# A hybrid transformer block: the first attention's rotated keys turned on VectorE through DRAM, two weight loads issued by ScalarE, input rows loaded a group earlier, and normalisation transposes of the feed-forward pinned in order

## The chip, the cores and the metric

The kernel runs on one core of a Trainium2 chip, in one launch. The metric is the device time of that launch in microseconds, lower is better. Three runs of the kernel before took 2479.9, 2481.11 and 2481.55 us; the median, 2481.11 us, is the time before. The profile is of one more execution, which took 2478.19 us.

Engines: PE (TensorE: matmuls, and transposes by a matmul with the identity), DVE (VectorE), ACT (ScalarE), POOL (GpSimd) and SP (SyncE, which here only issues DMAs). SBUF is the on-chip memory, with 128 partitions; PSUM holds what PE writes, in banks of 128 x 512 floats. All data are fp32.

## The reference

Four layers with residuals act on `x` of shape (4, 512, 512), that is 4 batches of 512 rows:

```python
x = x + attn_a(layernorm(x), Wq, Wk, Wv, Wo)      # "first attention"
x = x + ffn(layernorm(x), w1, w2, w3)             # ternary weights
x = x + attn_b(layernorm(x), codes, scales, ...)  # "second attention"
x = x + ffn(layernorm(x), w1, w2, w3)             # the same weights again
```

The change is in the first attention, and a little in the feed-forward. The first attention has 16 query heads and 4 key/value heads of 128:

```python
q, k, v = h @ Wq, h @ Wk, h @ Wv          # k, v repeated for 4 query heads each
o_gla = scan(S = S * exp(gl_t) + softmax(k)_t v_t;  o_t = softmax(q)_t S)
        # gl = log_sigmoid(k) / 16
sq, sk = rotary(q), rotary(k)
y = softmax(causal(sq @ sk.T / sqrt(128))) @ v
out = (0.5 * y + 0.5 * o_gla) @ Wo
```

## The kernel before, in words

**Groups and chunks.** The first attention works through 16 groups, one for each batch `b` and key head `g`, in the order `b`-major: group m has (b, g) = divmod(m, 4). A group has 4 chunks of 128 rows. So there are 64 chunks, and `step(n)` (L550) runs once for each chunk number n from -7 to 65. It is a software pipeline: in one step the parts of several chunks are traced, in the order in which L550 to L617 list them. With `m, p = divmod(n + 7, 4)`, `p` says at which quarter of the preparation of group m the step is. For a chunk c of a group, the parts are:

- `A` (L447): the query projection, 4 matmuls in PSUM tag `mm`, copied to `q_t` by ACT. `B` (L453): the decayed softmax of q (`qd`), its turning on its side, and the rotation (`qr`). `C` (L471): `qr` transposed by PE. `D(h)` (L482): scores of head h against the rotated keys `krT` in PSUM tag `sc`, masked maximum by DVE (L492), exponential by ACT (L495), division by ACT (L497), turning by DVE (L498); after head 3 the result is written to DRAM. `E` (L503) reads it back. `own` (L475) and `F` (L510) make the output, `G` (L522) multiplies it by Wo and adds it to the residual rows `xs` (L191, DVE).
- A group's preparation is spread over `part(m, p, half)` (L528): p = 0, 1 project k and v and start the gates; p = 2 `decays` (L405), in which DVE and POOL also make the rotated keys `kr` (L421 to 422) and then `kd`; p = 3 `transposes` (L426), in which PE transposes `kr` and `kd`, 4 blocks of 128 x 128 each (L362), and ACT copies both out of PSUM, `krT` with the factor 1/sqrt(128) (L428); p = 4 `states`. The chunk that first uses `krT` comes three steps after `transposes`.

**Turning through DRAM.** VectorE's transpose turns only blocks of 32 x 32. The kernel uses it on `qd` already: `turned` (one buffer) gets the turned blocks (L459), one DMA writes it to DRAM (`queries`, L461, 256 KB), and one step later four DMAs read it back (L468), each for the 32 partitions of one quarter, so that the blocks land transposed. The probabilities take the same way (L498, L501, L507).

**Loads.** SP issues nearly all DMAs, in one in-order queue. `load(b)` (L105) fetches the four tiles of input rows of batch b, at p = 0 of the last group of the batch before (L554 to 556: steps 5, 21 and 37). `load_wq` (L382) and `load_wo` (L386) fetch 1 MB each for a group; their tiles have one buffer, so they wait for the last matmul that reads the old weights.

**Layernorm.** `layernorm_steps` (L123) is a generator, advanced a bit at a time inside the steps: statistics of the rows by DVE (L132, L133), the scale by POOL and DVE (L138 to L145), the normalised rows `xn` (L160, one buffer), four PE transposes (L165) and a copy out. For the first attention, `normalise(b + 1)` starts one step after `load(b + 1)`. `halved` (L172) does the same for the two feed-forwards, with the result split in two fp32r halves; there the batch b + 1 is normalised while batch b is multiplied (L1086, L1100 to 1101).

**What sets the order.** The instructions are traced in program order, and a list scheduler then orders each engine's instructions by its own estimate of times: an instruction that it believes to be ready may be put ahead of others that were traced earlier. Two things hold it back. Inside the steps 0 to 63 PE's order is exactly the traced one (`manual_schedule`, L622), for the instructions traced there. And `in_place` (L79) pins one instruction behind whatever was traced before it on its engine. The order that comes out is fixed in the program; on the chip each engine's queue is in order, and an instruction that waits holds up those behind it. PSUM tags `mm` and `tp` have two banks, `sc` three.

Of the kernel before, what the change touches and what calls it, by code (L numbers as in the profile page):

```python
# [9 lines left out]
F32 = mybir.dt.float32  # L10
# [9 lines left out]
P = 128  # L20
B, S, C = 4, 512, 512
NC = S // P
# [52 lines left out]
def hybrid_block(ctx: ExitStack, tc: tile.TileContext, a: dict, out: bass.AP):  # L75
# [42 lines left out]
    def split(hi, lo, src, engine=nc.vector):  # L118

        nc.scalar.copy(hi, src)  # L120
        engine.tensor_tensor(lo, src, hi, ALU.subtract)

    def layernorm_steps(b, sink, tag="tp", apart=False):  # L123

        mv = lnp.tile([P, NC, 2], F32, tag="mv", name="mv")
        rstd = lnp.tile([P, NC], F32, tag="rstd", name="rstd")

        def moments(c):  # L130
            st = lnp.tile([P, 6], F32, tag="st", name="st")
            nc.vector.bn_stats(st, xs[b * NC + c])  # L132
            nc.vector.bn_aggr(mv[:, c, :], st)  # L133

        def scales(at):

            var = lnp.tile([P, NC], F32, tag="var", name="var")[:, at]
            nc.vector.tensor_scalar(var, mv[:, at, 1], LN_EPS, None, ALU.add)  # L138
            r = rstd[:, at]
            nc.gpsimd.tensor_tensor(r, var, power[:, : r.shape[1]], ALU.pow)  # L140
            t = lnp.tile([P, NC], F32, tag="newton", name="newton")[:, at]
            nc.vector.tensor_tensor(t, r, r, ALU.mult)
            nc.vector.tensor_tensor(t, t, var, ALU.mult)
            nc.vector.tensor_scalar(t, t, -0.5, 1.5, ALU.mult, ALU.add)
            nc.vector.tensor_tensor(r, r, t, ALU.mult)  # L145

        if not apart:
            for c in range(NC):
                moments(c)
                if c == 1:  # L150
                    yield
            scales(slice(0, NC))
        for c in range(NC):
            if apart:
                moments(c)
                scales(slice(c, c + 1))
            else:
                yield
            xn = lnp.tile([P, C], F32, tag="xn", name="xn", bufs=1)
            nc.vector.tensor_scalar(xn, xs[b * NC + c], mv[:, c, 0:1], rstd[:, c : c + 1], ALU.subtract, ALU.mult)  # L160
            if not apart:
                yield
            tp = bank(tag, [P, NK, P])
            for k in range(NK):
                nc.tensor.transpose(tp[:, k, :], xn[:, k * P : (k + 1) * P], ident)  # L165
            sink(c, tp)

    def layernorm(b, sink, tag="tp", apart=False):
        for _ in layernorm_steps(b, sink, tag, apart):
            pass  # L170

    def halved(pool, b):  # L172

        halves = [pool.tile([P, NK, S], F32R, tag=f"xn{n}", name=f"xn{n}") for n in ("hi", "lo")]
        return halves, layernorm_steps(b, lambda c, tp: split(*(h[:, :, c * P : (c + 1) * P] for h in halves), tp))

    def whole(pool, b):

# [130 lines left out]
    def first_attention_gentle(base, extra):  # L309
# [6 lines left out]
        with ExitStack() as st:  # L316
# [41 lines left out]
            def transposed(dst, src, engine):  # L358

                tp = bank("tp", [P, 4, P])  # L360
                for i in range(4):
                    nc.tensor.transpose(tp[:, i, :], src[:, i, :], ident)  # L362
                engine(dst, tp)

            xnTs = {}

            def normalise(b, apart=False):
# [4 lines left out]
            class Group:  # L372
# [8 lines left out]

                def load_wq(self):  # L382
                    self.wq = one.tile([P, NK, HG * D], F32, tag="wq", name="wq")
                    nc.sync.dma_start(self.wq, a["Wq"][:, self.g * HG * D : (self.g + 1) * HG * D].rearrange("(k p) n -> p k n", p=P))

                def load_wo(self):  # L386
                    self.wo = late.tile([P, HG, C], F32, tag="wo", name="wo")
                    nc.sync.dma_start(self.wo, a["Wo"][self.g * HG * D : (self.g + 1) * HG * D, :].rearrange("(h p) n -> p h n", p=P))

                def project(self, c):  # L390
                    acc = bank("mm", [P, 2, D])
# [13 lines left out]
                def decays(self):  # L405

                    dec = bank("mm", [P, NC, D])
                    halves = [one.tile([P, NC, D], F32R, tag=tag, name=f"gate{x}") for x, tag in (("hi", "held"), ("lo", "kd"))]
                    split(*halves, self.gate)
                    project(dec.rearrange("p c d -> p (c d)"), lambda i: until, lambda i: halves[i].rearrange("p c d -> p (c d)"), 2)  # L410

                    held = one.tile([P, NC, D], F32, tag="held", name="held")
                    nc.vector.tensor_scalar(held, dec, -2.0 * GENTLE * GATE_NORM, None, ALU.max)
                    self.down = two.tile([P, NC, D], F32, tag="down", name="down")
                    nc.scalar.activation(self.down, held, AF.Exp, scale=1.0 / GATE_NORM)
                    self.ends = two.tile([P, NC - 1], F32, tag="ends", name="ends")
                    for c in range(NC - 1):
                        nc.sync.dma_start(self.ends[:, c : c + 1], self.down[P - 1 : P, c, :])
                    n = self.g * B + self.b
                    nc.scalar.activation(held, held, AF.Exp, scale=-1.0 / GATE_NORM, accum_out=steep[:, n : n + 1])  # L420
                    self.kr = one.tile([P, NC, D], F32, tag="gate", name="kr")  # L421
                    rotate(self.kr, self.k_t, turn[:, :, 0:1, :], turn[:, :, 1:3, :])
                    self.kd = one.tile([P, NC, D], F32, tag="kd", name="kd")
                    softmax_decayed(self.kd, self.k_t, lambda c: held[:, c, :])

                def transposes(self):  # L426
                    self.krT = two.tile([P, S], F32, tag="krT", name="krT")
                    transposed(self.krT.rearrange("p (c t) -> p c t", c=NC), self.kr, lambda o, i: nc.scalar.mul(o, i, SCALE))  # L428
                    self.kdT = two.tile([P, NC, P], F32, tag="kdT", name="kdT")
                    transposed(self.kdT, self.kd, nc.scalar.copy)  # L430

# [11 lines left out]
            class Chunk:  # L443
# [9 lines left out]
                def B(self):  # L453
                    c = self.c
                    qd = one.tile([P, HG, D], F32, tag="qd", name="qd")
                    softmax_decayed(qd, self.q_t, lambda h: self.k.down[:, c, :])

                    turned = one.tile([P, 4, HG, 32], F32, tag="turned", name="turned")
                    nc.vector.transpose(turned.rearrange("p q h t -> p h q t"), qd.rearrange("p h (q j) -> p h q j", q=4))  # L459
                    self.queries = dram.tile([P, HG * D], F32, tag="queries", name="queries", bufs=3)  # L460
                    in_place(nc.sync.dma_start(self.queries, turned.rearrange("p q h t -> p (q h t)")))  # L461
                    self.qr = two.tile([P, HG, D], F32, tag="qr", name="qr")
                    rotate(self.qr, self.q_t, turn[:, c : c + 1, 0:1, :], turn[:, c : c + 1, 1:3, :])

                def L(self):
                    qdT = two.tile([P, 4, HG, 32], F32, tag="qdT", name="qdT", bufs=4)
                    for q in range(4):
                        in_place(nc.sync.dma_start(qdT[32 * q : 32 * (q + 1)].rearrange("j a h t -> j a (h t)"), self.queries.rearrange("(a j) (q x) -> q j a x", a=4, q=4)[q]))  # L468
                    self.qdT = qdT.rearrange("p a h t -> p h a t")

                def C(self):  # L471
# [10 lines left out]
                def D(self, h):  # L482
# [2 lines left out]
                    if h == 0:  # L485
                        self.turned = late.tile([P, HG * P * (3 + c % 2)], F32, tag=f"turned{c % 2}", name="turned")[:, : 4 * HG * 32 * n]
                    sc = bank("sc", [P, 4, 32 * n])
                    nc.tensor.matmul(sc.rearrange("p q (k j) -> p q k j", j=32), lhsT=self.qrT[:, h, :], rhs=self.k.krT.rearrange("p (k q j) -> p q k j", q=4, j=32)[:, :, :n, :], start=True, stop=True)  # L488
                    nm = two.tile([P, 1], F32, tag="nm", name="nm", bufs=4)
                    flat = sc.rearrange("p q x -> p (q x)")  # L490

                    nc.vector.tensor_tensor_reduce(sc, sc, causal[:, :, 32 * (3 - c) :], -1.0, 3e38, ALU.add, ALU.min, nm)  # L492
                    pr = two.tile([P, S], F32, tag="pr", name="pr", bufs=5)[:, : P * n]
                    den = two.tile([P, 1], F32, tag="den", name="den", bufs=4)
                    nc.scalar.activation(pr, flat, AF.Exp, bias=nm, scale=-1.0, accum_out=den)  # L495
# [54 lines left out]
            def step(n):  # L550
                nonlocal ln
                m, p = divmod(n + 7, NC)
                at = lambda i: chunks.get(n + i) if n + i < last else None
                if (m + 1) % KV == 0 and (m + 1) // KV < B:  # L554
                    if p == 0:
                        load((m + 1) // KV)
                    if p == 1:
                        ln = normalise((m + 1) // KV)
                    if p > 1:
                        next(ln)  # L560
# [514 lines left out]
    def feed_forward(base, last, first):  # L1075

        with ExitStack() as st:
# [5 lines left out]
            ws = [block((soon, soon) if f < 2 else pools, f) for f in range(NF)]  # L1083
            xn = first
            for b in range(B):
                ready, steps = halved(base, b + 1) if b + 1 < B else (None, iter(()))  # L1086
                hid = []
                for f, (w, _) in enumerate(ws):
                    xs12 = []
# [102 lines left out]
```

## Time and profile before

| | us |
|---|---|
| median of 3 runs | 2481.11 (2479.9 to 2481.55) |
| the profiled execution | 2478.19 |
| its span, first to last instruction | 2476.4 |
| PE busy in the span | 2427.4 (98%) |
| DVE, ACT, POOL busy | 1648.0 (67%), 1209.7 (49%), 387.7 (16%) |
| mean granted TensorE clock | 0.994 |
| first attention, from 0 to its last residual addition (L191) | 0 to 1053.3 |

How to read it: "busy" is the time in which an engine had an instruction under way; matmuls overlap a little with the next, so for PE the start of the next instruction says what one really costs. A timeline row gives the start in us, the duration in us, engine, line, operation, out<-in, and how many like instructions are merged in it (an fp32 matmul stands as two records, so four matmuls show as x8; a transpose stands as one). In square brackets stands how long the engine sat idle before the row, and what ended that. PE's clock is granted by a throttle; after an idle stretch the same matmuls can run slower for a while. SPq and ACTq are the DMAs that SP and ACT issue.

### The profile page before, as it was taken

The numbers are of one execution on the slowest core, as the hardware profiler recorded it, in microseconds if no ns is written. First come the engines' busy times: TensorE is split into PE (matmuls) and PEld (weight loads), VectorE is DVE, ScalarE is ACT, GpSimd is POOL, SyncE is SP. The second block draws the span as 40 slices with busy tenths as digits, with TensorE's granted clock in tenths as the row PEclk, the third lists the DMA queues.
The fourth block names the chain that finished last, engine by engine and source line by source line (L and its number), as shares of the span: only waits on it lengthen the run. The fifth ranks groups of instructions, "written<-read, shape, count | busy, mean of one in ns | idle before, by whom it ended". The sixth has DMA issues, their size and how long they took to land.

```text
span 2476.4 us, 28996 instructions
## 1 busy us (share of the span) xinstructions
PE 2427.4 (98%) x8552; PEld 1544.3 (62%) x8552; DVE 1648.0 (67%) x3816; ACT 1209.7 (49%) x3066; POOL 387.7 (16%) x424
## 2 busy tenths in 40 slices
PE   7999999999999999899999999999999999999998
PEld 4545555555555555477886666666666666668887
DVE  6778777887878888456558666666766666664332
ACT  5756665666666665233326554444444444432222
POOL 1222222122222222022223333100000000000000
PEclk9999999999999999899999999999999999999999
DMA  4667765776656655475436777544343434333000
GB/s 146 190 176 208 209 190 176 206 208 181 187 174 196 196 176 165 127 230 149 128 107 187 200 185 221 146 115 116 94 131 93 125 93 132 89 92 132 18 18 19
DMA packets 240615, 367.10 MB, mean 148 GB/s; under 512 B 41664, under 2 KB 126912, under 8 KB 234304
## 3 DMA queue, kind: packets, MB, share of 16 engines
q1 hardware_dynamic: 231088, 338.58, 48.2%
q0 software_dynamic: 7680, 25.17, 3.5%
q8 instruction: 71, 1.16, 0.2%
q10 hardware_dynamic: 1680, 1.39, 0.2%
q14 instruction: 96, 0.79, 0.1%
HBM read 209.53 MB, written 88.34 MB: 120 GB/s over the span
## 4 chain that ended last, share of the span: by engine, by line
PE 89%; DVE 5%; issue 2%; ACT 1%; DMA 1%; SPq 1%; POOL 1%; DVEq 0%; POOLq 0%; ACTq 0%
PE mm L186 44%; PE sc L186 13%; PE sc L888 9%; PE pv L518 5%; PE sc L488 5%; PE pv L922 4%; PE tp L922 4%; PE sc L478 2%; PE pv L516 1%; PE tp L362 1%; PE tp L165 1%; SPq L915 1%; DVE st L132 0%; DVE xn L160 0%; DMA prT<-turned 0%
## 5 line engine op out<-in xcount | busy, mean ns | idle before, releaser
L893 ACT ACTIVATE pr<-sc,nm 128x512 f32<-128x512 f32 x256 | 175.8, 687 | 302.6 <-DVE nm L890 259.2
L186 PE MATMUL sc<-xnhi,block 128*128 128x512 f32 x704 | 276.9, 393 | 2.1 <-ACT hT L1095 2.1
L186 PE MATMUL sc<-xnlo,block 128*128 128x512 f32 x704 | 274.3, 390 | 0.0
L888 PE MATMUL sc<-kT,qT 128*128 128x512 f32 x512 | 262.0, 594 | 0.6 <-ACT kT L870 0.6
L186 PE MATMUL mm<-xnhi,w 128*128 128x512 f32 x512 | 254.1, 496 | 0.0
L186 PE MATMUL mm<-wq,xnT 128*128 128x512 f32 x512 | 232.2, 596 | 4.1 <-DVE x L191 2.0
L186 PE MATMUL mm<-wo,oT 128*128 128x512 f32 x512 | 232.8, 598 | 1.1 <-ACT oT L520 0.7
L890 DVE TENSOR_REDUCE nm<-sc 128x1 f32<-128x512 f32 x256 | 174.9, 683 | 74.3 <-PE sc L888 72.1
L186 PE MATMUL mm<-xnlo,w 128*128 128x512 f32 x512 | 205.9, 402 | 0.0
L910 DVE STREAM_TRANSPOSE turned<-pr 128x512 f32<-128x512 f32 x256 | 173.4, 696 | 37.0 <-ACT pr L900 34.0
L343 POOL TENSOR_TENSOR sw<-q_t,turn 128x256 f32<-128x256 f32 x128 | 98.8, 792 | 510.6 <-ACT q_t L451 441.2
L900 ACT ACTIVATE pr<-pr,den 128x512 f32<-128x512 f32 x192 | 138.2, 722 | 82.6 <-DVE den L898 82.6
L488 PE MATMUL sc<-krT,qrT 128*128 128x512 f32 (+3 forms) x512 | 170.4, 433 | 2.2 <-ACT pr L495 2.2
L497 ACT ACTIVATE pr<-pr,den 128x128 f32<-128x128 f32 (+3 forms) x256 | 141.7, 558 | 48.2 <-DVE den L496 46.3
L186 PEld LDWEIGHTS mm<-wq,xnT 128*128 128x128 f32 x512 | 96.4, 191 | 109.9 <-issue 99.1
L495 ACT ACTIVATE pr<-sc,nm 128x128 f32<-128x128 f32 (+3 forms) x256 | 132.6, 519 | 65.2 <-DVE nm L492 55.5
L498 DVE STREAM_TRANSPOSE turned<-pr 128x128 f32<-128x128 f32 (+3 forms) x256 | 128.6, 504 | 47.4 <-ACT pr L497 43.0
L186 PEld LDWEIGHTS mm<-wo,oT 128*128 128x128 f32 x512 | 96.8, 192 | 101.3 <-issue 96.0
L186 PEld LDWEIGHTS sc<-xnhi,block 128*128 128x128 f32 x704 | 132.2, 188 | 31.1 <-ACT hT L1095 2.9
L186 PEld LDWEIGHTS sc<-xnlo,block 128*128 128x128 f32 x704 | 132.2, 188 | 27.7 <-issue 0.7
L518 PE MATMUL pv<-prT,v_t 128*128 128x512 f32 x320 | 147.8, 592 | 0.0
L888 PEld LDWEIGHTS sc<-kT,qT 128*128 128x128 f32 x512 | 95.8, 189 | 81.6 <-issue 63.5
(151 smaller groups left out, 4801.5 us busy)
## 6 DMA issues: line engine op xcount, KB each, us to landing
prT<-turned SPq DMA_DIRECT2D x1024, 64.0 KB, 2.0
w<-exact SPq DMA_DIRECT2D x32, 1024.0 KB, 5.3
wq<-in_Wq SPq DMA_DIRECT2D x16, 1024.0 KB, 5.7
wo<-in_Wo SPq DMA_DIRECT2D x16, 1024.0 KB, 5.9
queries<-turned SPq DMA_DIRECT2D x64, 256.0 KB, 2.3
qdT<-queries SPq DMA_DIRECT2D x256, 64.0 KB, 3.0
passed<-turned SPq DMA_DIRECT2D x16, 1024.0 KB, 4.3
prT<-passed SPq DMA_DIRECT2D x64, 256.0 KB, 5.9
```

The source lines that it names most:

```text
L186: nc.tensor.matmul(acc, lhsT=lhs(k), rhs=rhs(k), start=k == 0, stop=k == n - 1)
L488: nc.tensor.matmul(sc.rearrange("p q (k j) -> p q k j", j=32), lhsT=self.qrT[:, h, :], rhs=self.k.krT.rearrange("p (k q j) -> p q k j", q= ...
L495: nc.scalar.activation(pr, flat, AF.Exp, bias=nm, scale=-1.0, accum_out=den)
L497: nc.scalar.mul(pr, pr, den)
L498: nc.vector.transpose(self.turned.rearrange("p (q h x) -> p q h x", q=4, h=HG)[:, :, h, :], pr.rearrange("p (q x) -> p q x", q=4))
L518: nc.tensor.matmul(acc.rearrange("p h (a t) -> p h a t", a=4), lhsT=self.k.v_t[:, j, :], rhs=self.wts[:, :, :, j, :], start=j == c == 0, s ...
L888: nc.tensor.matmul(sc, lhsT=qTs[u][:, i * P : (i + 1) * P], rhs=kTs[u], start=True, stop=True)
L890: nc.vector.tensor_reduce(nm, sc, AX.X, ALU.max, negate=True)
L893: nc.scalar.activation(pr, sc, AF.Exp, bias=nm, accum_out=den)
L900: nc.scalar.mul(pr, pr, den)
L910: nc.vector.transpose(turns[u][:, :, i, :], pr.rearrange("p (q k) -> p q k", q=4))
L922: nc.tensor.matmul(accs[u].rearrange("p (n t) -> p n t", t=32), lhsT=v_ts[m, j][:, h * D : (h + 1) * D], rhs=prTs[u].rearrange("p a i (k t ...
```

## The change

- **Rotated keys.** `kr` is no longer transposed by PE. `decays` turns it in blocks on DVE into `turned` (the same single buffer that the queries use) and has SP write it to DRAM; `transposes` has SP read it back with four DMAs. The two helpers `blocks_to_dram` and `quarters` hold what L459 to L461 and L467 to L468 did for the queries, and serve both. `krT` is thereby stored by quarters, and is no longer scaled: the factor goes into the masked maximum of L492, which takes -1/sqrt(128) where it took -1. The DRAM tag `queries` has four buffers in place of three.
- **Wq and Wo** of the first attention are issued by ACT, each pinned behind the ACT instruction traced before it, in place of SP.
- **Input rows** of the next batch are loaded at p = 0 of the second last group of a batch: steps 1, 17 and 33 in place of 5, 21 and 37.
- **Transposes held.** In the feed-forwards, the first of the four transposes of each chunk of the next batch's normalisation is pinned behind the PE instruction traced before it.

```diff
-    def layernorm_steps(b, sink, tag="tp", apart=False):
+    def layernorm_steps(b, sink, tag="tp", apart=False, place=lambda i: i):
...
             for k in range(NK):
-                nc.tensor.transpose(tp[:, k, :], xn[:, k * P : (k + 1) * P], ident)
+                t = nc.tensor.transpose(tp[:, k, :], xn[:, k * P : (k + 1) * P], ident)
+                if k == 0:
+                    place(t)
...
-    def halved(pool, b):
+    def halved(pool, b, **kw):
...
-        return halves, layernorm_steps(b, lambda c, tp: split(*(h[:, :, c * P : (c + 1) * P] for h in halves), tp))
+        return halves, layernorm_steps(b, lambda c, tp: split(*(h[:, :, c * P : (c + 1) * P] for h in halves), tp), **kw)
...
+            def blocks_to_dram(src):
+
+                turned = one.tile([P, 4, 4, 32], F32, tag="turned", name="turned")
+                nc.vector.transpose(turned.rearrange("p q n t -> p n q t"), src.rearrange("p n (q j) -> p n q j", q=4))
+                to = dram.tile([P, 4 * P], F32, tag="queries", name="queries", bufs=4)
+                in_place(nc.sync.dma_start(to, turned.rearrange("p q n t -> p (q n t)")))
+                return to
+
+            def quarters(dst, src):
+
+                for q in range(4):
+                    in_place(nc.sync.dma_start(dst[32 * q : 32 * (q + 1)].rearrange("j (a x) -> j a x", a=4), src.rearrange("(a j) (q x) -> q j a x", a=4, q=4)[q]))
...
-                    nc.sync.dma_start(self.wq, a["Wq"][:, self.g * HG * D : (self.g + 1) * HG * D].rearrange("(k p) n -> p k n", p=P))
+                    in_place(nc.scalar.dma_start(self.wq, a["Wq"][:, self.g * HG * D : (self.g + 1) * HG * D].rearrange("(k p) n -> p k n", p=P)))
...
-                    nc.sync.dma_start(self.wo, a["Wo"][self.g * HG * D : (self.g + 1) * HG * D, :].rearrange("(h p) n -> p h n", p=P))
+                    in_place(nc.scalar.dma_start(self.wo, a["Wo"][self.g * HG * D : (self.g + 1) * HG * D, :].rearrange("(h p) n -> p h n", p=P)))
...
-                    self.kr = one.tile([P, NC, D], F32, tag="gate", name="kr")
-                    rotate(self.kr, self.k_t, turn[:, :, 0:1, :], turn[:, :, 1:3, :])
+                    kr = one.tile([P, NC, D], F32, tag="gate", name="kr")
+                    rotate(kr, self.k_t, turn[:, :, 0:1, :], turn[:, :, 1:3, :])
+                    self.keys = blocks_to_dram(kr)
...
-                    self.krT = two.tile([P, S], F32, tag="krT", name="krT")
-                    transposed(self.krT.rearrange("p (c t) -> p c t", c=NC), self.kr, lambda o, i: nc.scalar.mul(o, i, SCALE))
+                    krT = two.tile([P, S], F32, tag="krT", name="krT")
+                    quarters(krT, self.keys)
+                    self.krT = krT.rearrange("p (q k j) -> p q k j", q=4, j=32)
...
-                    nc.vector.tensor_tensor_reduce(sc, sc, causal[:, :, 32 * (3 - c) :], -1.0, 3e38, ALU.add, ALU.min, nm)
+                    nc.vector.tensor_tensor_reduce(sc, sc, causal[:, :, 32 * (3 - c) :], -SCALE, 3e38, ALU.add, ALU.min, nm)
...
+                if p == 0 and (m + 2) % KV == 0 and (m + 2) // KV < B:
+                    load((m + 2) // KV)
                 if (m + 1) % KV == 0 and (m + 1) // KV < B:
-                    if p == 0:
-                        load((m + 1) // KV)
...
-                ready, steps = halved(base, b + 1) if b + 1 < B else (None, iter(()))
+                ready, steps = halved(base, b + 1, place=in_place) if b + 1 < B else (None, iter(()))
```

More of the change, by code (lines that the diff above doesn't have):

```diff
@@ L456, in B @@
                     softmax_decayed(qd, self.q_t, lambda h: self.k.down[:, c, :])
[L458 to L461, printed above, removed]
+                    self.queries = blocks_to_dram(qd)
                     self.qr = two.tile([P, HG, D], F32, tag="qr", name="qr")
@@ L466, in L @@
                     qdT = two.tile([P, 4, HG, 32], F32, tag="qdT", name="qdT", bufs=4)
-                    for q in range(4):
-                        in_place(nc.sync.dma_start(qdT[32 * q : 32 * (q + 1)].rearrange("j a h t -> j a (h t)"), self.queries.rearrange("(a j) (q x) -> q j a x", a=4, q=4)[q]))
+                    quarters(qdT.rearrange("p a h t -> p (a h t)"), self.queries)
                     self.qdT = qdT.rearrange("p a h t -> p h a t")
@@ L487, in D @@
                     sc = bank("sc", [P, 4, 32 * n])
-                    nc.tensor.matmul(sc.rearrange("p q (k j) -> p q k j", j=32), lhsT=self.qrT[:, h, :], rhs=self.k.krT.rearrange("p (k q j) -> p q k j", q=4, j=32)[:, :, :n, :], start=True, stop=True)
+                    nc.tensor.matmul(sc.rearrange("p q (k j) -> p q k j", j=32), lhsT=self.qrT[:, h, :], rhs=self.k.krT[:, :, :n, :], start=True, stop=True)
                     nm = two.tile([P, 1], F32, tag="nm", name="nm", bufs=4)
                     flat = sc.rearrange("p q x -> p (q x)")
-                    nc.vector.tensor_tensor_reduce(sc, sc, causal[:, :, 32 * (3 - c) :], -1.0, 3e38, ALU.add, ALU.min, nm)
+                    nc.vector.tensor_tensor_reduce(sc, sc, causal[:, :, 32 * (3 - c) :], -SCALE, 3e38, ALU.add, ALU.min, nm)
                     pr = two.tile([P, S], F32, tag="pr", name="pr", bufs=5)[:, : P * n]
```

## The prediction

> **What bounds the kernel now.** I read the shares by engine first, then the chain that ended last by engine, then a 50 us stretch of the first attention by windows, because the edits lie in that stage.
>
> ```profile
> PE 2427.4 (98%) x8552; PEld 1544.3 (62%) x8552; DVE 1648.0 (67%) x3816; ACT 1209.7 (49%) x3066; POOL 387.7 (16%) x424
> PE 89%; DVE 5%; issue 2%; ACT 1%; DMA 1%; SPq 1%; POOL 1%; DVEq 0%; POOLq 0%; ACTq 0%
> 250.00:300.00 50.00, 50.00 (x161) 27.75 (x160) 38.29 (x101) 31.45 (x96) 9.97 (x11) 1.00 0.73 212
> ```
>
> PE is the bound, in this stage too: from 250 to 300 us PE is busy 50.00 of 50, DVE 38.29, ACT 31.45. So an edit gains only what it takes from PE's queue, or from the places where PE stands. To find these I went through PE's timeline. The starts of the query projections (mm<-wq,xnT) mark the steps; undisturbed, four steps take 15.27 + 15.26 + 13.16 + 17.67 = 61.36 us, again and again. The places in the first attention, after its start-up, where PE stood 1.7 us or more, with the DVE and SP rows that belong to them (634.90 is the third change of batch):
>
> ```profile
> 129.76 0.69 DVE L132 BATCH_NORM_STATS2 st<-x 128x6 f32<-128x512 f32 x1 [1.59 <-DMA x<-in_hidden]
> 131.15 0.69 DVE L132 BATCH_NORM_STATS2 st<-x 128x6 f32<-128x512 f32 x1 [0.48 <-DMA x<-in_hidden]
> 140.95 0.68 DVE L191 TENSOR_TENSOR x<-x,mm 128x512 f32<-128x512 f32 x1
> 141.69 3.78 PE L186 MATMUL mm<-wkv,xnT 128*128 128x256 f32 x8 [4.79 <-DVE x L191]
> ...
> 384.81 0.69 DVE L132 BATCH_NORM_STATS2 st<-x 128x6 f32<-128x512 f32 x1 [1.46 <-DMA x<-in_hidden]
> 396.50 5.40 PE L186 MATMUL mm<-wq,xnT 128*128 128x512 f32 x8 [2.02 <-DVE x L191]
> ...
> 634.90 0.66 DVE L132 BATCH_NORM_STATS2 st<-x 128x6 f32<-128x512 f32 x1
> 696.95 3.70 PE L186 MATMUL mm<-wq,xnT 128*128 128x512 f32 x8 [1.75 <-DVE state L440]
> ...
> 1007.23 0.40 SPq L388 DMA_DIRECT2D wo<-in_Wo  x1
> 1008.59 0.84 PE L165 MATMUL tp<-ident,xn 128*128 128x128 f32 x4 [1.87 <-DVE xn L160]
> 1011.62 1.09 PE L165 MATMUL tp<-ident,xn 128*128 128x128 f32 x4 [2.19 <-DVE xn L160]
> 1017.77 5.99 PE L186 MATMUL mm<-wo,oT 128*128 128x512 f32 x8
> ```
>
> The reader is to see three things. Twice DVE stood in the layernorm statistics until the input rows had landed, so its residual addition L191 came late, so a `mm` bank came free late, and PE stood 4.79 and 2.02 us. After each, eight matmuls ran slow: 3.78 in place of 1.89 us, 5.40 in place of 3.60. At the end of the stage PE took up the next batches' layernorm transposes and stood before four-packs of them, with the last Wo multiplications queued behind.
>
> **Keys off PE.** Sixteen groups lose four transposes each.
>
> ```profile
> 366.01 0.60 PE L362 MATMUL tp<-ident,kr 128*128 128x128 f32 x4
> 366.45 0.60 PE L362 MATMUL tp<-ident,kd 128*128 128x128 f32 x4
> 366.89 3.60 PE L186 MATMUL mm<-wo,oT 128*128 128x512 f32 x8
> L459 DVE STREAM_TRANSPOSE turned<-qd 128x512 f32<-128x512 f32 x64 | 43.9, 686 | 0.0
> queries<-turned SPq DMA_DIRECT2D x64, 256.0 KB, 2.3
> qdT<-queries SPq DMA_DIRECT2D x256, 64.0 KB, 3.0
> ```
>
> The four hold PE's queue from 366.01 to 366.45, that is 0.44 us. Group 0 is in the start-up, where PE stands anyway; the other 15 give 15 x 0.44 = **6.6 us**.
>
> The group rows give 275 ns for one such transpose, and the Trainium skill ("TensorE: Matmul & The Clock Gate", Part 4) has about 275 ns in one kernel too. By that price the 64 would be worth 17.6 us; the starts above, 0.11 us apart, decide against it.
>
> What is added: 16 turnings on DVE at 0.686 us = 11.0 us; 16 writes at 0.34 us of SP's time and 64 reads at about 0.45. ACT loses 16 copies of 0.577 us. The data are needed three steps (46 us) after the reads start, against 2.3 + 3.0 us of landing, and the write lies one step before the reads. So nothing new waits on the path. The 0.69 us on DVE fall in the step of p = 2, where DVE is idle 1.3 to 2.4 us in the groups I summed, with 3 to 4 us idle in the step after. The price not shown is the one `turned` buffer: in the group at 290 us the queries' turning ends at 296.5, its write is issued at 296.55 and lands 2.3 us later, at about 298.9; kr is done at 297.1. If nothing else is put in between, DVE stands 1.8 us. Bounds for the sixteen: 0 (hidden in idle time, since POOL, ACT and PSUM banks have slack there: the next `mm` bank that hangs on L191 is wanted some 7 us after it), and 16 x 1.8 = 29 us (all of it passed on to PE). Nearest is the row of idle DVE time: I take **1 us of loss**.
>
> The Trainium skill ("VectorE: DVE Perf Modes", Rules for kernel authors) speaks against this edit: a 128 x 128 transpose belongs on TensorE where PSUM will do, and VectorE turns 32 x 32 blocks only. If DVE were the bound, that rule's sum would be 11.0 - 6.6 = 4.4 us of loss; the windows row, PE 50.00 against DVE 38.29, says otherwise.
>
> **Input rows sooner.** The step with the first stall lasts 23.01 us in place of 15.27, the two around the second 17.97 + 17.24 in place of 15.27 + 15.26: 7.7 + 4.7 = 12.4 us lost. Some 0.4 us of it are the quantiser's small matmuls, the rest stall and slow matmuls: 12. With the rows there four steps earlier DVE does not stand (1.59 + 0.48 and 1.46 us); DVE's work remains (four statistics, some 3.5 us). The third change of batch shows that case: there the rows had landed in time, no statistic waited, and that step of PE lasted 15.27. So I take **11 us**; the lower bound is DVE's waiting alone, 3.5. The third change's own excess (steps 15.65, 14.90 and 20.74 against 15.26, 13.16 and 17.67, less four layernorm packs of 0.44: 3.4) comes from DVE work that no edit removes: I take 0, bounds 0 and 3.4. Of the moved step, SP's four issues (2.3 us) now come at p = 0 of the group before, ahead of the same reads; 0, as SP is 1% of the chain, and PE's attention output of one to three chunks had its operand 10 us and more ahead.
>
> **Wq and Wo from ACT.** SP loses 32 issues of 0.40 us, ACT gains as many. ACT's own small loads at the start held its queue 0.42 to 0.62 us. Twice that in a group of 61 us, where ACT is idle some 20, is hidden, and the copies it lost are 0.58. Wq's wait (the last projection) has been met by the copy of q before it on ACT; Wo's by PE's order. If the wait were not met, the exponentials behind it would stand. Bounds -3 and +3; I take 0.
>
> **Transposes held.** From 996 to 1018 us six packs of four run on PE for the two next batches, 24 transposes. Without them PE reaches the Wo multiplication of chunk 60 at about 1006.5. That must wait for Wo: issued at 1007.23, landing 5.9 us later (median) at 1013.1; from ACT, about 1 us sooner, 1012. A stall of 5.5 us follows, so slow matmuls again (5.99). From there all is a chain: the last score's probabilities, two DMAs, output, Wo: 1052.6 - 1017.8 = 34.8 us. So the stage ends 1017.8 - 1012 = 5.8 us sooner. But the six packs, 6 x 0.44 = 2.6 us, now lie in the feed-forward, where PE is full. Net **3 us**, bounds -2.6 (the chain is not moved) and +9 (Wo in time, full clock). In the second feed-forward a 0.80 us wait of the same kind (at 2230) goes: **+0.5**.
>
> **Start-up.** PE's wait for kr (2.24 us at 32.3) ends in a wait for kd, which DVE now makes up to 0.69 us later; krT must be back by 43.9 and can be by about 41; but SP's first weight loads stand behind its reads. Bounds -3 and +2; 0.
>
> Sum: 6.6 - 1 + 11 + 3 + 0.5 = **20 us**, 2478.2 to 2458 by the profiled execution. That ran 2.9 us below the median, so 2481.1 - 20 = **2461**.
>
> **Rivals.**
> - *The statistics cost as much without the wait.* DVE's 3.5 us of statistics still stand before L191, and PE's gap only shrinks by what DVE waited: 3.5 in place of 11, and the tail gives 0 to 3: gain 9 to 13, about **2470**. For it: DVE had a backlog of over 6 us and waited only 2.07. Against it: the third change of batch. 24%.
> - *The tail is not shortened* (Wo or the last DMAs bind it) and PE pays the packs: 20 - 3 - 2.6 = 14: **2467**. For it: the chain of DMAs after the last score. 14%.
> - *More:* the third change's excess goes too and the tail gives 9: 20 + 3 + 6 = 29: **2452**. 12%.
> - *DVE becomes the bound (slower).* The place is p = 2 of each group: kr's turning waits for the one `turned` buffer, 1.8 us, plus 0.69 of its own: 2.5. It decides once this passes the 1.3 to 2.4 us of idle DVE time and reaches PE; if all of it does, 16 x 2.5 = 40, less the other gains of 20 to 25: **2498**. The stalls shown here make it possible: 2.02 us of standing were followed by 1.8 us of slow matmuls. 8%.
> - *It does not do what it says:* the scheduler, by its own times, puts the early statistics or the reads where they hold up DVE or SP, and the gain is spent: within 5 us of **2481**. 7%.
>
> **How the numbers follow.** The forecast has 35%; its own range is 2456 to 2466. A measurement of this kernel tells about 0.2% (5 us) from no change. Faster: 35 + 24 + 14 + 12 = 85%. Same: 7%. Slower: 8%. The range leaves out the last two cases and gains above 31: 2450 to 2475.
>
> **What would show it.** After: no tp<-ident,kr; 16 more turnings on DVE; undisturbed groups of 60.9 us in place of 61.36; the steps of the two changes of batch at 15 to 16 us, with no DVE wait for input rows; no layernorm packs from 996 to 1018, and the last L191 of the stage some 23 us earlier. Wrong if groups stay at 61.4 or more with PE standing for DVE at p = 2, if L132 runs early but L191 is late all the same, or if the feed-forward loses more than the 2.6 us.

## The result, and the profile after

The changed kernel took 2505.77 us (median of 5 runs, 2505.24 to 2510.54); five runs of the kernel before have a median of 2479.9 (2477.12 to 2481.55). The ratio is 1.0112, 95% interval 1.0101 to 1.0123: slower by 1.1%. The forecast was 2461, so it was wrong in sign. The profiled execution took 2508.02 us, with a span of 2505.7. In the changed kernel the project matmul is now L188, the residual addition L193, `blocks_to_dram` L367 to 374 (turning L370, write L372), `states` L457 and 458, `load_wo` L403.

First the page of the changed kernel, shares by engine and the chain that ended last, and then the window that was shown of before (PE, PEld, DVE, ACT and POOL busy in 50 us, then PE's clock):

```profile
PE 2435.0 (97%) x8488; PEld 1539.5 (61%) x8488; DVE 1651.5 (66%) x3832; ACT 1201.6 (48%) x3050; POOL 388.3 (15%) x424
PE 72%; DVE 14%; ACT 4%; DMA 4%; issue 4%; SPq 1%; POOL 1%; DVEq 0%; POOLq 0%; ACTq 0%
```

```profile
250.00:300.00 50.00, 47.41 (x144) 25.60 (x143) 37.04 (x97) 28.54 (x84) 6.57 (x8) 0.97 0.64 187
```

PE has fallen from 89% of the chain to 72%, and DVE has risen from 5% to 14%. In the window PE stands for 2.59 of 50 us, where it stood for none, though DVE is no busier (37.04 against 38.29). So DVE is not full; PE waits for its order. The list of waits from 100 to 960 us (engine, line, what it waited for: us in total, times, longest) names it:

```profile
DVE turned L370 <- DMA queries<-turned: 23.9, 12, 2.5
...
PE mm L188 <- DVE state L457: 22.4, 11, 2.6
```

One of these places in the timeline of the changed kernel:

```profile
499.38 0.70 DVE L370 STREAM_TRANSPOSE turned<-qd 128x512 f32<-128x512 f32 x1
...
513.87 0.67 DVE L370 STREAM_TRANSPOSE turned<-kr 128x512 f32<-128x512 f32 x1
514.56 0.35 SPq L372 DMA_DIRECT2D queries<-turned  x1
516.69 0.71 DVE L370 STREAM_TRANSPOSE turned<-qd 128x512 f32<-128x512 f32 x1 [2.16 <-DMA queries<-turned]
...
519.52 0.25 DVE L457 TENSOR_TENSOR state<-state,mm 128x128 f32<-128x128 f32 x1
519.82 3.70 PE L188 MATMUL mm<-wq,xnT 128*128 128x512 f32 x8 [2.56 <-DVE state L457]
```

Read it downwards. The keys are turned 14.5 us after the query turning at 499.38, just ahead of the next one. That next one wants the same `turned` buffer and stands 2.16 us until the keys' write has landed. The state sums of `states`, queued behind it on DVE, come late (the last at 519.52), so their `mm` bank comes free late, and PE stands 2.56 us before the query projection. In ten of the fourteen groups after the start-up the step that ends there lasts 19.4 to 20.0 us, where 17.67 less the four transposes is 17.23; in six groups the step after it, with slow matmuls, lasts 17.0 to 17.1 in place of 15.27.

Where the time went, with marks taken from both traces (query projection of the same chunk at 105.93 and 113.74; last query projection at 980.30 and 1009.33; last L191/L193 at 1052.61 and 1074.38; first matmul `xnhi,block` of the second feed-forward at 2207.55 and 2231.83; ends of the spans):

| stretch | before | after | difference |
|---|---|---|---|
| start-up | 105.93 | 113.74 | +7.8 |
| 56 chunks, 14 groups | 874.37 | 895.59 | +21.2 |
| end of the first attention | 72.31 | 65.05 | -7.3 |
| first feed-forward, second attention | 1154.94 | 1157.45 | +2.5 |
| second feed-forward | 268.85 | 273.87 | +5.0 |

In the start-up (changed kernel, timeline):

```profile
46.51 0.39 ACTq L403 DMA_DIRECT2D wo<-in_Wo  x1
46.90 0.43 SPq L224 DMA_DIRECT2D w<-in_w1T  x1
...
53.33 0.74 ACT L233 ACTIVATE w<-w 128x640 f32<-128x640 f32 x1 [5.70 <-DMA w<-in_w1T]
...
55.90 0.80 PE L188 MATMUL mm<-gatehi,until 128*128 128x512 f32 x1 [6.66 <-ACT gatehi L120]
```

Group 0's Wo, 1 MB, which SP used to issue at 5.78 us, goes out at 46.51, right ahead of a piece of weights for the quantiser. That piece, 320 KB, takes 6.4 us to land (median of its kind 4.0), ACT stands 5.70 us for it, and PE 6.66 us for ACT.

At the end of the attention (changed kernel, PE):

```profile
1022.64 0.60 PE L165 MATMUL tp<-ident,xn 128*128 128x128 f32 x4
1026.90 3.60 PE L188 MATMUL mm<-wo,oT 128*128 128x512 f32 x8
1038.99 6.53 PE L188 MATMUL mm<-wo,oT 128*128 128x512 f32 x8 [3.34 <-DMA wo<-in_Wo]
```

No transposes for later batches hold the last Wo multiplications; one PE pack is left and waits for nothing. But PE still stands 3.34 us for the last Wo, and its matmuls then run slow (6.53 in place of 3.60).

### The profile page after: what moved, and what is told of

It is laid out like the page before. It is cut to its first block, busy times and chain, and to the rows that moved or that the text cites. A ratio compares the mean times of both kernels' runs of the same rounds, so it can differ in the third digit from the quotient of the medians.

```text
span 2505.7 us, 28958 instructions
## 1 busy us (share of the span) xinstructions
PE 2435.0 (97%) x8488; PEld 1539.5 (61%) x8488; DVE 1651.5 (66%) x3832; ACT 1201.6 (48%) x3050; POOL 388.3 (15%) x424
## 4 chain that ended last, share of the span: by engine, by line
PE 72%; DVE 14%; ACT 4%; DMA 4%; issue 4%; SPq 1%; POOL 1%; DVEq 0%; POOLq 0%; ACTq 0%
PE mm L188 37%; PE sc L188 10%; PE sc L900 9%; PE tp L934 4%; PE pv L934 4%; PE sc L500 3%; PE pv L530 2%; DVE qd L358 2%; DVE turned L510 1%; DVE qr L346 1%; ACT pr L509 1%; ACT pr L507 1%; DVE sc L504 1%; DMA queries<-turned 1%; PE sc L490 1%
## 5 line engine op out<-in xcount | busy, mean ns | idle before, releaser
L188 PE MATMUL sc<-xnhi,block 128*128 128x512 f32 x704 | 277.3, 394 | 4.6 <-ACT hT L1107 2.8
L188 PE MATMUL sc<-xnlo,block 128*128 128x512 f32 x704 | 275.2, 391 | 0.0
L188 PE MATMUL mm<-wq,xnT 128*128 128x512 f32 x512 | 242.5, 618 | 22.5 <-DVE state L457 22.4
L188 PE MATMUL mm<-xnhi,w 128*128 128x512 f32 x512 | 254.1, 496 | 0.0
L188 PE MATMUL mm<-wo,oT 128*128 128x512 f32 x512 | 234.9, 602 | 6.5 <-DMA wo<-in_Wo 5.8
L188 PE MATMUL mm<-xnlo,w 128*128 128x512 f32 x512 | 205.8, 402 | 0.0
L188 PEld LDWEIGHTS mm<-wq,xnT 128*128 128x128 f32 x512 | 99.2, 198 | 137.8 <-issue 105.4
L188 PEld LDWEIGHTS mm<-wo,oT 128*128 128x128 f32 x512 | 97.4, 193 | 108.9 <-issue 96.5
L188 PEld LDWEIGHTS sc<-xnhi,block 128*128 128x128 f32 x704 | 132.2, 188 | 34.9 <-ACT hT L1107 4.0
L188 PEld LDWEIGHTS sc<-xnlo,block 128*128 128x128 f32 x704 | 132.2, 188 | 27.7 <-issue 1.0
```

The source lines that it names most:

```text
L188: nc.tensor.matmul(acc, lhsT=lhs(k), rhs=rhs(k), start=k == 0, stop=k == n - 1)
```

## The experiments

**Theory.** The keys share one `turned` buffer with the queries; in the order that comes out, the keys' turning stands directly ahead of a queries' turning, which then waits for the keys' write. **Rivals:** the loads from ACT; the held transposes; DVE's sixteen added turnings as such; the traffic on SP's queue. Ratios are against the kernel before on the same chip, with the 95% interval.

**1. Two buffers** (`two_turned`).

```diff
-                turned = one.tile([P, 4, 4, 32], F32, tag="turned", name="turned")
+                turned = one.tile([P, 4, 4, 32], F32, tag="turned", name="turned", bufs=2)
...
-                low = pool.tile([P, 6 * P], BF16, tag="low", name="low")[:, : w.shape[1]]
+                low = pool.tile([P, 6 * P], BF16, tag="low", name="low", bufs=1)[:, : w.shape[1]]
```

> The changed kernel with two `turned` buffers in place of one (the quantiser's `low` tile goes from two buffers to one to make room; both its writer and its reader are DVE). Theory 'one buffer': the keys' turning shares one buffer with the queries' turning, DVE stands about 2.2 us per group for the keys' write, and PE stands or runs slow after it. From the traces the loss of the groups is 21.8 (attention longer) - 7.5 (start-up) + 12 (batch changes repaired) + 6.6 (transposes gone) = 33 us; with two buffers it goes: about 2473 us, and DVE no longer waits for queries<-turned. Rival 'DVE's added work': the 16 turnings of 0.69 us are what delays the state: time stays within 8 us of the changed kernel, 2498 or more. Rival 'loads from ACT': 2500 or more, since nothing of the loads is touched.

Measured: 2469.95 us, 0.9963 [0.9948, 0.9977]; as the theory said, some 3 us better. Timeline, and the group of the query projections on the page (busy, mean ns | idle before), first in the changed kernel and then with two buffers:

```profile
482.33 0.66 DVE L370 STREAM_TRANSPOSE turned<-qd 128x512 f32<-128x512 f32 x1
484.08 0.69 DVE L370 STREAM_TRANSPOSE turned<-kr 128x512 f32<-128x512 f32 x1
...
499.15 0.67 DVE L370 STREAM_TRANSPOSE turned<-qd 128x512 f32<-128x512 f32 x1
```

```profile
L188 PE MATMUL mm<-wq,xnT 128*128 128x512 f32 x512 | 242.5, 618 | 22.5 <-DVE state L457 22.4
L188 PE MATMUL mm<-wq,xnT 128*128 128x512 f32 x512 | 231.4, 595 | 0.5 <-DVE state L457 0.5
```

The same DVE work is there; only the buffer counts differ (the quantiser's `low` gave up one to make room). The keys' turning now follows the queries' by 1.75 us in place of 14.5, no turning waits for a write, and half of the steps at p = 3 last 17.23 us (the one shown here is among two that stayed at 17.6 to 17.7). The 56 chunks take 856.83 us: 38.8 less than in the changed kernel, 17.5 less than before.

**2. The keys without the rest** (`keys_alone`): the kernel before, with `blocks_to_dram(kr)`, `quarters(krT, ...)` and the scale moved, and nothing else.

> The kernel before with the rotated keys alone turned through DRAM (one `turned` buffer, Wq and Wo on SP, rows as before, no held transposes). Theory 'one buffer': 2480 + 33 - 6.6 = about 2506 us, steps of p = 3 some 19.6 us and the batch-change stalls still there. Rival 'loads from ACT': keys cost nothing, 2473 to 2480.

Measured: 2567.58 us, 1.0351 [1.0326, 1.0377]; far more than the theory gave. Timeline:

```profile
183.52 1.89 SPq L433 DMA_DIRECT2D ends<-down  x3
196.11 0.70 DVE L370 STREAM_TRANSPOSE turned<-kr 128x512 f32<-128x512 f32 x1
196.83 0.35 SPq L372 DMA_DIRECT2D queries<-turned  x1
...
203.09 0.40 SPq L399 DMA_DIRECT2D wq<-in_Wq  x1
...
211.41 5.74 PE L188 MATMUL mm<-wq,xnT 128*128 128x512 f32 x8 [10.03 <-DMA wq<-in_Wq]
```

```profile
PE mm L188 <- DMA wq<-in_Wq: 67.3, 8, 10.0
```

SP issues nothing from 185.4 to 196.83: the keys' write is pinned in its queue where it was traced, and DVE turns the keys only at 196.11. Wq, in the same queue, goes out 6 us later still, and PE stands 10.03 us for it. Eight such waits make 67.3 us, as the list of waits from 100 to 960 us has it. So the late turning has a second price on SP, which the changed kernel does not pay because its Wq is on ACT.

**3. Is that so?** `keys_two_alone` is `keys_alone` with the edit of experiment 1. `keys_wq_from_act` is `keys_alone` with `load_wq` on ACT.

> The kernel before with the rotated keys alone turned through DRAM, but with two `turned` buffers (and one `low`); Wq and Wo stay on SP. Theory 'one buffer': with two buffers the scheduler puts the keys' turning where it was traced, so the keys' write no longer stands at the head of SP's queue, Wq behind it is issued in time, and DVE doesn't wait: 2480 - 6.6 + 3 (start-up) = about 2476. Rival 'SP's queue': the sixteen writes and 64 reads on SP hold up Wq whatever the buffers: 2500 or more.

Measured: 2476.55 us, 0.9982 [0.9973, 0.9992]; as expected, so neither SP's traffic nor DVE's added work costs what the late turning did.

> As keys_alone (one `turned` buffer, rows as before, no held transposes, Wo on SP), but with Wq issued by ACT. Theory: 67 us of the 88 that keys_alone lost were PE's waiting for Wq, which stood on SP behind the keys' write; off that queue they go, and what is left is DVE's wait for the buffer: 2500 to 2515. Rival 'the DMAs of the keys are in each other's way': 2540 or more.

Measured: 2502.93 us, 1.0103 [1.0075, 1.013]; as expected in time. No wait for Wq is left, and DVE's wait for the buffer is (20.5 us in 13 waits). But PE stands only 5.5 us in 3 waits for the state sums here, against 22.4 in the changed kernel, and 7.8 us in 7 waits for Wo, which is on SP (100 to 960 us). So the run shows that Wq's place on SP cost what it was said to; that the rest of its loss is DVE's wait is not shown.

**4. All but the keys** (`no_keys`): the changed kernel with `transposed(krT, kr)` of before.

> The changed kernel without its first part: the rotated keys transposed by PE as before; loads from ACT, earlier rows and held transposes stay. Theory: all of the loss sits in the keys' part. From the traces of the single parts: batch changes -11, end of the attention -7.5, start-up +4 to +7, feed-forwards +2.7 and +3: about 2472, so the keys' part costs some 34 us in the changed kernel. Rival 'loads from ACT or held transposes': 2490 or more.

Measured: 2469.67 us, 0.996 [0.9946, 0.9974]. Against 1.0112 the keys' part costs 1.5%, some 37 us. With two buffers it costs nothing against this, and gains nothing that the medians can tell (2469.95 and 2469.67 us). In the two profiles the 56 chunks are 8.5 us shorter in `two_turned` than in `no_keys` (856.83 against 865.34), and 2.6 of that go in the start-up, where the projection at 110.83 without the keys is at 113.45 with them.

**5. The sharing or the place?** `one_buffer_pinned` pins the keys' softmax behind the keys' turning. `one_buffer_traced_later` keeps the one buffer but calls `blocks_to_dram(kr)` half a step later, ahead of the next `B`; `keys_traced_later` does the same to `keys_alone`.

```diff
-                    self.keys = blocks_to_dram(kr)
+                    self.kr = kr
...
+                if p == 3 and m in groups:
+                    groups[m].keys = groups[m].blocks(groups[m].kr)
                 if z:
                     z.B()
```

> The changed kernel with its one `turned` buffer, and the keys' softmax (its maximum on DVE) pinned behind the keys' turning, so that the keys' turning no longer stands right ahead of the queries' turning: the normalisations of kd and qd, some 2.5 us of DVE, lie between. Theory 'the wait is for the write of the keys, 2.2 us, and decides because nothing lies between': DVE's wait goes, most of the 35 us come back, 2475 to 2485; what is left is the later kd. Rival 'one buffer costs wherever it is shared, or the later place of the turning costs by itself': 2495 or more.

Measured: 2626.59 us, 1.0588 [1.0571, 1.0606]. A miss that tells nothing of the wait's price: DVE no longer waited for the write, but `kd` came late, and PE, whose order is fixed, stood before its transposes for 102.6 us in 12 waits (100 to 960 us).

> The changed kernel, one `turned` buffer, with the keys' turning and write traced half a step later, as in keys_traced_later. Theory: as with two buffers, about 2470 (2468 to 2478): what costs is the place that the one buffer gave the keys' turning, directly ahead of the queries', and of the write in SP's queue, not the sharing. Rival: DVE waits for the write wherever it stands: 2495 or more.

Measured: 2478.98 us, 0.9999 [0.9985, 1.0012]: 28 of the 37 us are back with one buffer.

```profile
505.77 0.67 DVE L370 STREAM_TRANSPOSE turned<-kr 128x512 f32<-128x512 f32 x1
...
512.67 0.67 DVE L370 STREAM_TRANSPOSE turned<-qd 128x512 f32<-128x512 f32 x1
```

With 6.9 us between the two, DVE has no wait for the write from 100 to 1080 us, and the steps of p = 3 are 17.23 us in most groups. So most of the price is that of the place, and the sharing alone need not cost. The remaining 9 us against `two_turned` lie in a later start (2.1 us) and in PE waits of up to 1.6 us for Wo and for ACT's copies in some steps; why these came is not settled.

> As keys_alone, but the keys' turning and write are traced half a step later, right ahead of the next chunk's B; Wq stays on SP, and in SP's order it now stands ahead of the keys' write. Still one `turned` buffer; DVE's order has some 14 rows between the keys' turning and the queries'. Theory 'place in the queues': Wq is in time and DVE has work between the two turnings: 2475 to 2490. Rival 'one buffer costs wherever it is shared': 2505 or more.

Measured: 2502.49 us, 1.0095 [1.0066, 1.0123], between theory and rival and nearer to the rival, but not for its reason: DVE has no wait for the write from 100 to 1080 us here. Of the 88 us 63 are back, and PE's 67.3 us for Wq have become one wait of 0.39. What is left shows as waits for Wo (9.7 us) and ACT's copies, and the three changes of batch (one step of 21.5 to 22.4 us in each); it was not followed further.

**6. The other three parts alone.** `rows_alone`, `act_issue_alone` and `held_alone` are the kernel before with that one part of the diff (and the four `queries` buffers).

> The kernel before with the input rows loaded four steps sooner, nothing else. Theory (the part of the forecast that the trace of the changed kernel seems to bear out): 11 to 12 us less, about 2468. Rival 'the statistics cost as much without the wait': 3.5 us less, about 2476.

Measured: 2473.4 us, 0.9971 [0.9959, 0.9982], between the two.

> The kernel before with Wq and Wo issued by ACT, nothing else. Theory: the start-up loses some 7 us (Wo's 1 MB is issued at 46 us in place of 6 us, and the quantiser's piece behind it lands late, with ACT's queue behind that), and the rest is unchanged: 2484 to 2490. Rival 'loads from ACT are the main loss': 2495 or more. Forecast on record: 2477 to 2483.

Measured: 2473.99 us, 0.9978 [0.9968, 0.9987]: faster, where a loss was expected.

> The kernel before with the feed-forward's transposes held, nothing else. Forecast on record: 3.5 us less, about 2476. Theory from the trace of the changed kernel: the six packs move into the first feed-forward (2.6 us there), the second feed-forward starts later (the changed kernel lost 5 us there), and the end of the attention gives at most 3 us back: 2482 to 2486. Rival: the 5 us in the second feed-forward came from something else: 2476 to 2480.

Measured: 2480.02 us, 0.9997 [0.9988, 1.0007]: no change, neither the forecast's gain nor the loss expected now; the last L193 is 2.0 us sooner, and the span still ends 2.4 us later.

In `rows_alone` the three changes of batch are 14.4 us shorter, but three other steps are longer. One of them:

```profile
317.24 0.69 DVE L132 BATCH_NORM_STATS2 st<-x 128x6 f32<-128x512 f32 x1 [0.84 <-DMA x<-in_hidden]
...
329.24 0.68 DVE L193 TENSOR_TENSOR x<-x,mm 128x512 f32<-128x512 f32 x1
329.97 3.70 PE L188 MATMUL mm<-wq,xnT 128*128 128x512 f32 x8 [1.89 <-DVE x L193]
```

The statistics have been drawn forward with the rows; DVE does them, waiting 1.20 us, in this step, and here too L193 comes late and PE stands 1.89 us.

> As rows_alone, with the layernorm statistics of the first attention pinned behind the DVE instruction traced before them, so that the earlier rows don't draw them forward. Theory: in rows_alone the statistics ran some two steps sooner than they were traced, waited 1.20 us for the rows at 317 to 319 us and made L193 late there (17.37 in place of 15.27 us; 16.57 and 14.44 in place of 15.26 and 13.16 at the next change of batch); pinned, these 4.7 us come back: about 2469. Rival: the four row loads themselves cost it, by holding up what is behind them on SP: 2473.

Edit: `in_place` round the `bn_stats` of the first attention. Measured: 2492.55 us, 1.0053 [1.0036, 1.0069], against both. Pinned, the statistics come too late: PE stood 6.8 to 7.0 us before the layernorm transposes of each change of batch. It therefore does not tell whether the statistics or the loads cost those steps.

**7. A better version.** `two_turned_early_wo` is `two_turned` without held transposes and with group 0's Wq and Wo on SP, unpinned; `early_wo_rows_before` also loads the rows where they were; `keys0_on_pe` also transposes group 0's keys on PE.

> The changed kernel with two `turned` buffers, without held transposes, and with group 0's Wq and Wo issued by SP, free to be put early as in the kernel before; ACT issues the other groups'. Theory: the start-up wins back about 4 us (Wo's 1 MB no longer lands ahead of the quantiser's piece), the feed-forwards 4 to 6: from 2470 to about 2461. Rival: the start-up is set by the keys' way through DRAM, 2466 or more.

Measured: 2466.38 us, 0.9943 [0.9925, 0.9961]: the rival's time, though not for its reason alone. The query projection at 73.19 in `two_turned` is at 70.03, 3.2 us sooner; but without held transposes the end of the attention is 5.5 us longer (69.9 against 64.3 by the marks of the table), and the stretches behind it are only 3.5 us shorter.

> As two_turned_early_wo, but with the input rows loaded where the kernel before loads them. Theory: with Wq and Wo off SP's queue the rows land in time anyway (with loads from ACT alone the steps of the first two changes of batch were 6.5 and 3.4 us shorter), so the earlier load is worth little and costs 3 us in the start-up: 2458 to 2463, no slower than with early rows. Rival: the early rows are worth the 11 us of the forecast: 2470 or more.

Measured: 2466.59 us, 0.9945 [0.9928, 0.9961], no slower than with early rows: with the loads on ACT and two buffers, the earlier rows are worth nothing that can be told.

> As early_wo_rows_before, with group 0's rotated keys transposed by PE as before (PE stands there anyway), the other fifteen through DRAM. Theory: the 4.5 us that the start-up still loses against the kernel before are the keys' way through DRAM (read back in 2.9 us, after a write of 2.7 us, in a stretch where PE waits for them): about 2462. Rival: they come from the loads: 2466.

Measured: 2465.03 us, 0.9936 [0.9919, 0.9952], the lowest of all, but nearer to the rival: the query projection that was at 70.24 us is at 68.36, 1.9 us sooner and not 4.5, and 2.8 us behind the kernel before. What holds that rest was not found.

## Why the prediction was wrong

**The step that failed** is the price of the one `turned` buffer under "Keys off PE": "Nearest is the row of idle DVE time: I take 1 us of loss", with bounds 0 and 29. Against the kernel with two buffers it measured 38.8 us over the 14 groups (895.59 - 856.83): 23.4 in the steps of p = 3, 11.1 in the steps after them, and 4.2 in the last three, where PE stood 2.45 us for Wo. Three things in it were wrong.

- The place. The working had the turning at p = 2 right behind the rotation, with DVE standing 1.8 us there. With the one buffer the scheduler put it 14.5 us later, directly ahead of the next queries' turning. The line "if nothing else is put in between" named the condition and went no further: the front of this document says that the order comes from a scheduler, so the place of a new instruction that wants a busy buffer was itself an unknown with a price.
- What is queued behind. The cover that was counted on was the `mm` bank that hangs on L191, wanted some 7 us later. At the real place the state sums stand behind the wait, and their bank is wanted at once by the query projection: 2.16 us of DVE, with the keys' turning of 0.67 ahead of them, became 2.56 us of PE.
- The bound. 16 x 1.8 left out that PE's standing is followed by slow matmuls (1.8 us in six groups), a row that the prediction itself had shown.

The "slower" rival was this mechanism, given 8%: wait for the one buffer, passed on to PE. That its 40 us are close to the 38.8 is in part luck: it counted 2.5 us in sixteen groups, where PE stood in eleven places and ran slow behind six of them. Its place was wrong, and its gains too large by the start-up. Of the signs of being wrong the first came nearest: most groups last 63 to 66 us with PE standing for DVE, but at p = 3. The trace could have raised its chance: DVE's idle 1.3 to 2.4 us at p = 2 did not cover 2.5.

The Trainium skill ("VectorE: DVE Perf Modes", Rules for kernel authors) puts a 128 x 128 transpose on TensorE where a PSUM destination will do. The changed kernel (1.0112) did lose against PE's transposes (`no_keys`, 0.996), but not by the sum that was tried with that rule: DVE was not full, and with two buffers (0.9963) the same turnings cost nothing.

**The other terms.**

- *Keys off PE, +6.6, and input rows, +11:* near, once the buffer is repaired: the 56 chunks then gain 17.5 us against the kernel before. In ten of the fourteen groups the step at p = 3 is 0.44 us shorter, as forecast; the three groups with a change of batch are 15.5 us shorter in all. In the changed kernel DVE did not wait for input rows once from 100 us on. Alone the rows gave 0.29%, about 7 us; and loads from ACT alone shortened the first two changes of batch by 6.5 and 3.4 us as well. The gain at the changes of batch belonged to both edits, and the prediction gave it to one.
- *Wq and Wo from ACT, 0, bounds -3 and +3:* alone 0.22% faster, some 5.5 us, above the bounds.
- *Start-up, 0, bounds -3 and +2:* +7.8. That Wo's load is now pinned behind ACT's instructions, and so leaves at 46.51 in place of 5.78, was in the diff and was not priced. Putting group 0's Wq and Wo back on SP gave 3.2 us (query projection 70.03 against 73.19), and group 0's keys on PE another 1.9; where the rest went stays open.
- *Transposes held, +3:* the end of the attention gave 7.3 (forecast 5.8), the first feed-forward with the second attention lost 2.5 (forecast 2.6); near. By the same marks the end of the attention lasts 68.8 us with held transposes alone, 69.9 with the loads from ACT alone and 65.4 with both and without the keys (72.31 before): 3.5 us, 2.4 and 6.9. So about a third of the gain is that of the loads from ACT.
- *Second feed-forward, +0.5:* -5.0. The cause is open. With held transposes alone the stretch took 271.4 us against 268.85; but over all the profiles it took 270.9 to 274.6 us with held transposes and 268.9 to 273.2 without, so one pair of profiles does not tell.

Sum by the runs: 17.5 - 38.8 - 7.8 + 7.3 - 2.5 - 5.0 = -29.3, the difference of the spans.

## What to carry to other kernels

When an edit adds an instruction that reuses a single buffer, price two things: the wait, and where a scheduler will put the instruction because of that wait; then name what stands behind it on its own engine and what pinned DMA stands behind it in the issuing queue. A second buffer of 2 KB per partition was worth 36 us here, more than all the gains of the change. And measure parts both alone and in the whole: two parts repaired the same stall, and one part cost 88 us alone and 37 in company.

## What the runs showed of the hardware that was not expected

- PE's standing can be followed by slow matmuls, and how long it stood does not tell when. Of nine waits of 1.97 to 2.59 us for the state sums in the changed kernel, six were followed by a query projection of 5.3 to 5.4 us in place of 3.70, the shortest of the nine among them, and three were not, one of them of 2.56 us. The granted clock (the number after the five engines) shows it, here behind the wait of 2.07 us that ended at 583.09 and behind that of 2.56 us that ended at 519.82:

```profile
585.00:587.00 2.00, 2.00 (x4) 0.94 (x3) 0.72 (x2) 0.61 (x1) 1.26 (x1) 0.50 0.73 234
522.00:524.00 2.00, 2.00 (x6) 0.95 (x5) 1.27 (x3) 0.61 (x2) 0.00 (x0) 1.00 0.52 166
```

- The mean granted clock of the profiled executions is lower where PE stood longer: 0.994 in the kernel before and `two_turned`, 0.988 in the changed kernel, 0.977 in `keys_alone`, 0.967 in `one_buffer_pinned`.
- In the start-up of the changed kernel a 320 KB load that SP issued 0.39 us behind ACT's 1 MB load of Wo took 6.4 us to land. The same load took 6.3 us in `two_turned`, with Wo 0.4 us ahead of it too, and 3.7 us in `two_turned_early_wo` and `early_wo_rows_before`, where Wo had gone out early.
